# Moving a matmul chain forward, splitting a normalization root in two, and asking for weights on ScalarE's queue

## The chip, the cores and the metric

The kernel runs on one core of a Trainium2 chip. The metric is the device time of one execution in microseconds (us), as the median of several runs. TensorE (PE) does the matrix products, VectorE (DVE), ScalarE (ACT) and GpSimd (POOL) the elementwise work, and SyncE (SP) issues most DMAs.

## The reference

Everything is float32. `x` is 2 x 1024 tokens of 512 features.

```python
xn = layernorm(x)                                # over the 512 features
K  = s4_kernel(Lambda, p, q, B, Ct, step, 512)   # 512 values, real
s  = irfft(rfft(xn, 1024) * rfft(K, 1024))[:512] + D * xn   # causal convolution along the features
h1 = xn @ w1.T + 2 * (xn @ A1.T) @ B1.T          # hidden size 1376, LoRA rank 16
h3 = xn @ w3.T + 2 * (xn @ A3.T) @ B3.T
g  = silu(h1) * h3
f  = g @ w2.T + 2 * (g @ A2.T) @ B2.T
out = x + s * silu(f)
```

## The kernel before

The 2048 tokens are four blocks of TB = 512, each of four tiles of 128. Blocks 0 and 1 form super-block sb 0, blocks 2 and 3 form sb 1. Features lie on the partitions after a transpose on TensorE (`transpose`, pass L332; its copies out of PSUM are L340, L342 and L343 on ScalarE). The hidden units are cut into 11 chunks: five pairs of 128-unit chunks (NPAIR = 5) and a last one of 96.

The first half, h1, h3 and the gate, is done with Strassen-Winograd products: a 2 x 2 block product takes seven products instead of eight, at the price of sums of weights and of tokens. For a pair this is done at two levels, so there are seven chains of seven steps each. The steps of a chain have the numbers 1, 6, 2, 7, 5, 3, 4; each product (L812) writes one of the PSUM banks `x`, `w`, `y`. `Chain.step` snapshots bank `x` on ScalarE (L832) after steps 6 and 5, copies it to bank `w` after step 1 (L850), and adds bank `y` on VectorE (L836). `got` then combines the chain's results with those of other chains (L926, on VectorE or GpSimd), `Gate` applies silu (L885, ScalarE) and the product (L893, GpSimd), and `store_g` writes the result to DRAM by SyncE's queue (L864). The intermediate values lie in rotating buffers: `value("s")` has 10 and `value("c")` has 4; the pair's sums lie in `ua_one` and others.

The sums that the products need are these. `outer_weight_sums` (L486) and `inner_weight_sum` (L498) add blocks of weights, `outer_token_sum` (L374) and `inner_token_sum` (L387 to L393) blocks of tokens, all on VectorE with both operands in SBUF. The LoRA term is not a separate pass: `lora_product` (L429) multiplies the two factors into PSUM, and `merge` (L439, VectorE) adds them to the loaded weight. `load_pair` (L448) loads a pair's weights with four DMAs, two of `w1T` and two of `w3T`.

The normalization needs a mean, a variance and a reciprocal root for each token. Block 2's statistics are made by VectorE (L252, L253), block 3's by ScalarE (`act_sums` L259, `act_squares` L270) with small steps on GpSimd (L265, L266, L279). `pool_root` (L289 to L302) is a chain of 14 small GpSimd operations that gives scale and shift for blocks 2 and 3 together, and `normalize` applies them to a tile on ScalarE (L321) or on GpSimd (L325).

The order is written out by hand: `at(place, what)` puts an event on a heap, and all events are issued in order of place. One unit of place is about one TensorE product, `add_chain(n, ...)` puts a chain into slot n, that is at 7 n plus the places of its steps, and `after(delay, what)` adds an event behind the current one. Each engine works off its instructions in the order in which they were issued, and SyncE its DMA requests too, each behind the waits of those before it.

The last phase (out of the scope of most of the change) multiplies by w2 and the convolution. `conv_product` makes the causal 512 x 512 Toeplitz product of a 128-token tile from blocks of 128 columns (L986); the fp32 product of one block is two passes of TensorE.

Of the kernel before, what the change touches and what calls it, by code (L numbers as in the profile page):

```python
# [12 lines left out]
F32 = mybir.dt.float32  # L13
# [4 lines left out]
P = 128  # L18
# [89 lines left out]
def s4_gated_ffn(  # L108
# [59 lines left out]
    def bank(tag, borrow=False):  # L168

        i = turn[tag]  # L170
        if not borrow:
            turn[tag] = 1 - i
        return psum.tile([P, 512], F32, tag=f"{tag}{i}", name=tag, bufs=1)

    def aux():
        return bank("aux")
# [36 lines left out]
    ]  # L213

    def value(tag="s"):
        return upool.tile([P, TB], F32, tag=tag, name=tag, bufs={"s": 10, "c": 4}[tag])


    events, now = [], [0.0]
# [219 lines left out]
        nc.vector.scalar_tensor_tensor(to, ps, LORA_SCALE, to, mult, add)  # L439


    def load_pair(c):
        w = wpool.tile([P, 8, 2, 2, P], F32, tag="w", name="w")
        for v, src in enumerate((w1T, w3T)):
            for half in range(2):
                slot = (1, 2, 0, 3)[2 * v + half]
                rows = src[half * HALF : (half + 1) * HALF, PAIR_AT[c] : PAIR_AT[c] + 2 * P]
                nc.sync.dma_start(  # L448
                    out=w[:, slot].rearrange("p k m h -> p k (m h)"),
                    in_=rows.rearrange("(k p) h -> p k h", p=P),  # L450
                )
        return w
# [8 lines left out]
    def merge_half(w, half, v, ps):  # L461
        merge(w[:, (1, 2, 0, 3)[2 * v + half]].rearrange("p k m h -> p (k m h)"), ps[v])

    def merge_whole_pair(c, w, first=None, delays=(1.15, 2.3, 4.3, 4.4)):

        ps = [first or [bank("y", True), bank("w", True)], [bank("aux"), bank("aux")]]
        for half in range(2):
            for k in range(2):
                for v in range(2):
                    n = slice(half * 2 * P, (half + 1) * 2 * P)  # L470
                    lora_product(
                        ps[k][v][:, n], 2 * k + v, 2 * half + k, PAIR_AT[c], 2 * P, half == 0
                    )
        for (k, v), when in zip(((0, 0), (0, 1), (1, 0), (1, 1)), delays):
            to = w[:, (slice(1, 3), slice(0, 4, 3))[v], k].rearrange("p s m h -> p s (m h)")
            from_ = ps[k][v].rearrange("p (s n) -> p s n", s=2)
            after(when, lambda to=to, from_=from_: merge(to, from_))
# [418 lines left out]
    def last_chain(ab, sb):  # L896
        a, gate = ab, Gate(LASTR, LAST, sb)

        def pairs(i):
            n = B_AT[i]  # L900
            b = xr[:, n, sb] if n < 3 else xt[:, n - 3, sb]
            return [(a[A_AT[i]][:, k, :], b[:, k, :]) for k in range(2)]

        def got(o, c):
            if o < 20:
                gate.put(o, value("c")[:LASTR, :], c)
            else:
                gate.put(o, c)

        return Chain(pairs, LASTR, lambda o: value(), got, 1, 2 if sb == 0 else 1)  # L910

    def pair_chains(c, w, s, order):


        st = {}

        def at(name, o):
            key, n = (name + "_one", o - 11) if o < 20 else (name + "_three", o - 21)
            if key not in st:
                st[key] = upool.tile(  # L920
                    [P, 2, TB], F32, tag=key, name=key, bufs=2 if key == "ua_three" else 1
                )
            return st[key][:, n, :]

        def plus(o, to, a, b):
            (nc.vector if o < 20 else nc.gpsimd).tensor_tensor(to, a, b, add)  # L926

        def chain(j):
            gate = (
                Gate(P, 2 * c + (j in (5, 4)), int(j in (5, 3))) if j in (2, 5, 3, 4) else None  # L930
            )
            early3 = j == 3 and order.index(3) < order.index(5)
            if early3:
                st["early3"] = (gate, {})

            def pairs(i):
                return [(weight_operand(w, s, i, j), token_operand(i, j))]

            def keep(o):
                if j == 1 or j == 7 and o > 20:  # L940
                    return at("ua" if j == 1 else "u3", o)
                return value()

            def got(o, m):
                ua = at("ua", o)
                if j == 1:
                    if o < 20:
                        nc.scalar.copy(ua, m)
                elif j == 6:
                    plus(o, ua, ua, m)  # L950
                elif j == 7:
                    plus(o, at("u3", o), ua, m)
                elif early3:
                    held = st["early3"][1]
                    held[o] = m
                    if o < 20:
                        held[o] = value("c")
                        nc.scalar.copy(held[o], m)
                else:
                    if j == 5:  # L960
                        plus(o, ua, ua, m)
                    t = value("c") if o < 20 else m
                    plus(o, t, ua if j in (2, 3) else at("u3", o), m)
                    gate.put(o, t)
                    if j == 5 and "early3" in st:
                        g3, held = st["early3"]
                        plus(o, held[o], held[o], ua)
                        g3.put(o, held[o])

            return Chain(pairs, P, keep, got, 0.7 if (c, j) == (NPAIR - 1, order[5]) else 0)  # L970

        return [chain(j) for j in order]
# [6 lines left out]
    def conv_product(lhs, x01, x12, sb, tok, tag):  # L979
# [18 lines left out]
        m = work.tile([P, DIM], F32, tag="m", name="m", bufs=2)  # L998
        nc.scalar.copy(m[:, : 3 * P], shared[:, : 3 * P])
        nc.scalar.copy(m[:, 3 * P :], shared[:, :P])  # L1000
        mul(y, 0, x0, k0, True)
        mul(y, 3, x0, k3)
        mul(y, 1, x01[sb][:, tok], k2)
        mul(y, 2, x12[sb][:, tok], k1)
        mul(y, 3, x321, k0)
# [65 lines left out]
    mv = norm_tile(1)  # L1071
    norm_stats(1, range(NTT))
    norm_root(mv, 1)
    mv_late = norm_tile(2, 3)
    ab_last = last_operands(w_last, s_last)


# [25 lines left out]
    add_chain(3, lambda: last_chain(ab_last, 1), PLACES)  # L1103
    for n in range(2, 7):

        add_chain(n + 2, pair_chain(0, n), AT_T2 if n == 2 else PLACES)
    for c in range(1, NPAIR):
        for n in range(7):

            hurry = (c, n) in ((NPAIR - 2, 6), (NPAIR - 1, 4))  # L1110
            places = SOON if hurry else PLACES
            if (c, n) == (NPAIR - 1, 5):
                places = (*PLACES[:-1], (4, 13.5))
            add_chain(2 + 7 * c + n, pair_chain(c, n), places)
    at(-10, lambda: normalize(1))
    at(-9.9, lambda: last_sums(w_last, s_last))
    at(-10.5, lambda: ps_pair.append(pair_products(0, 1, [aux(), aux()])))
# [13 lines left out]
    for tt in range(NTT):  # L1131
        at(-0.4 + 0.1 * tt, lambda tt=tt: norm_stats(2, (tt,)))
        at(-1.4 + 0.1 * tt, lambda tt=tt: act_sums(3, tt))
        at((-0.3, -0.2, 1.7, 1.8)[tt], lambda tt=tt: act_squares(3, tt))
    at(-0.9, lambda: act_means(3))
    at(1.9, lambda: act_variances(3))
    at(6.9, lambda: pool_root(mv_late, 2, 3))
    at(7.7, lambda: normalize(2))
    at(8, lambda: normalize(3, (0,)))
    for n, place in enumerate((12.1, 12.8, 13.7, 14.4)):  # L1140
        b, i = divmod(n, 2)
        at(place, lambda b=b, i=i: transpose(2 + b, range(2 * i, 2 * i + 2)))
    for name, when in ((3, 15.7), (2, 15.9), (1, 21.2), (4, 21.4)):
        at(when, lambda name=name: outer_token_sum(1, name))
    at(18, other_factors)
    at(22.5, spill)
    for name, when in ((1, 12.7), (2, 13.4), (4, 14), (3, 30.5)):
        at(when, lambda name=name: inner_weight_sum(w_pair[0], s_pair[0], name))
    for name, raw, when, *half in (
        (3, True, 21.6),  # L1150
        (2, True, 22.8),
        (3, False, 24.2),
        (2, False, 30.2),
        (1, True, 34.4),
        (1, False, 37.5, 0),
        (1, False, 40.3, 1),
        (4, True, 47.6),
        (4, False, 50.2, 0),
        (4, False, 52.3, 1),
    ):  # L1160
        at(when, lambda of=(name, raw, *half): inner_token_sum(*of))

    for c in range(NPAIR):
        t0 = 14 + 49 * c

        def ready(j):

            n = orders[c].index(j)
            return 7 * (n + (2 if c == 0 and n > 1 else 0)) + (0 if c == 0 else t0) + 13.3

        if c + 1 < NPAIR:
            nx = c + 1
# [2 lines left out]
                return lambda: what(nx, w_pair[nx], *args)  # L1175

            if c > 0:
                at(t0 + 7.5, lambda nx=nx: w_pair.update({nx: load_pair(nx)}))
            t1 = t0 + (24 if c == 0 else 16)
            if c == 0:  # L1180
                at(
                    5.7,
                    lambda nx=nx: merge_whole_pair(
                        nx, w_pair[nx], [bank("w"), bank("w")], (4.1, 4.2, 4.8, 5.8)
                    ),
                )
            else:
                at(t0 + 15.6, step(merge_whole_pair))
            for n, name in enumerate((3, 2, 1, 4)):
                at(  # L1190
                    14.5 + 0.2 * n if c == 0 else t1 + 8.5 + 1.5 * n,
                    lambda nx=nx, name=name: outer_weight_sums(w_pair[nx], (name,)),
                )
            for name, when in (
# [462 lines left out]
```

## Time and profile before

| | us |
|---|---|
| median of 3 runs | 441.27 (441.01 to 441.75) |
| profiled execution | 442.36 |
| its span in the trace | 440.6 |

The granted TensorE clock is 0.999. The profile is of one execution. A row of a group gives line, engine, operation, output and input names, shape and count; the timeline gives start and duration in us, and in square brackets the idle time just before the row and what ended it. DVE, ACT, POOL and SP are the engines above, `SPq` is SyncE issuing a DMA, and `PEld` is the load of a weight into TensorE. Busy times of the engines, in shares of the span: PE 98%, DVE 72%, POOL 48%, ACT 33%. DMA moves 53.6 MB, 122 GB/s on average.

### The profile page before, as it was taken

To read this page: it belongs to the slowest core of one execution; us is meant where nothing else is said; L and a number is where in the kernel's file an instruction comes from. 1 tells how busy PE (TensorE), PEld (TensorE's weight loads), DVE (VectorE), ACT (ScalarE), POOL (GpSimd) and SP (SyncE) were. 2 spreads that over 40 slices of the span, in tenths; PEclk is the share of its full clock that TensorE was granted. 3 is DMA by queue.
4 is the path that set the end of the run, shared out by engine and by line. 5 is a ranking of instruction groups with operands and counts; after the bars stand their busy time and mean duration, and the time that the engine had idled before them with its cause. 6 is when DMAs were issued, how large, how long until landed. Compare 5 with 4: busy or idle time off the path is not lost.

```text
span 440.6 us, 5150 instructions
## 1 busy us (share of the span) xinstructions
PE 433.3 (98%) x1696; PEld 268.0 (61%) x1696; DVE 317.9 (72%) x519; ACT 144.8 (33%) x298; POOL 212.8 (48%) x174
## 2 busy tenths in 40 slices
PE   8999999999999999999999999999999999999996
PEld 7535334443444444444443446888898999999996
DVE  5889999955885687468745796979786885653234
ACT  3767242453255324532453242211101212112121
POOL 2539177994689468945894468400000122222221
PEclk9999999999999999999999999999999999999999
DMA  8920304025002500250045426395901842322211
GB/s 257 368 76 19 138 1 149 24 71 162 31 25 86 154 24 25 89 170 25 24 131 205 160 95 216 94 361 193 345 31 73 289 136 95 144 95 97 76 68 48
DMA packets 35465, 53.60 MB, mean 122 GB/s; under 512 B 4688, under 2 KB 21520, under 8 KB 35312
## 3 DMA queue, kind: packets, MB, share of 16 engines
q1 hardware_dynamic: 35088, 52.69, 35.7%
q10 hardware_dynamic: 352, 0.60, 0.4%
q8 instruction: 13, 0.21, 0.2%
q14 instruction: 12, 0.10, 0.1%
HBM read 33.88 MB, written 19.40 MB: 121 GB/s over the span
## 4 chain that ended last, share of the span: by engine, by line
PE 89%; DVE 7%; DMA 2%; ACT 1%; issue 1%; SPq 0%; POOL 0%; DVEq 0%; POOLq 0%; ACTq 0%
PE x L812 43%; PE y L812 23%; PE w L812 12%; PE aux L986 4%; PE w L986 2%; PE w L1047 1%; DMA w<-in_w1T_dram 1%; DVE xt L374 1%; DVE w L486 1%; DVE s L498 1%; DVE w L439 1%; PE y L429 1%; PE y L585 1%; PE aux L767 1%; DVE aux L1372 1%
## 5 line engine op out<-in xcount | busy, mean ns | idle before, releaser
L1375 POOL TENSOR_TENSOR o<-o,xin 128x512 f32<-128x512 f32 (+1 forms) x17 | 23.2, 1366 | 133.0 <-DVE o L1374 128.1
L893 POOL TENSOR_TENSOR s<-c,s 128x512 f32<-128x512 f32 (+1 forms) x44 | 64.1, 1464 | 15.4 <-ACT c L885 13.0
L832 ACT COPY s<-x 128x512 f32<-128x512 f32 (+1 forms) x54 | 31.5, 584 | 84.4 <-PE x L812 84.3
L812 PE MATMUL x<-t_in,s 128*128 128x512 f32 (+1 forms) x148 | 55.4, 501 | 0.0
L836 DVE TENSOR_TENSOR s<-s,y 128x512 f32<-128x512 f32 (+1 forms) x54 | 36.1, 680 | 14.7 <-PE y L812 8.8
L926 POOL TENSOR_TENSOR s<-ua_three,s 128x512 f32<-128x512 f32 x20 | 32.0, 1602 | 25.0 <-DVE s L836 24.8
L812 PEld LDWEIGHTS x<-t_in,s 128*128 128x128 f32 x148 | 26.6, 190 | 23.3 <-issue 11.5
L926 POOL TENSOR_TENSOR ua_three<-ua_three,s 128x512 f32<-128x512 f32 x20 | 30.6, 1528 | 13.9 <-DVE s L836 13.9
L812 PE MATMUL y<-t_in,s 128*128 128x256 f32 (+1 forms) x108 | 35.9, 459 | 0.9 <-DVE w L439 0.9
L1397 ACT COPY z<-x 128x256 f32<-128x256 f32 x24 | 8.8, 371 | 70.2 <-PE x L812 70.2
L885 ACT ACTIVATE c<-c 128x512 f32<-128x512 f32 x40 | 25.2, 632 | 14.2 <-DVE c L926 14.2
L926 POOL TENSOR_TENSOR s<-u_three,s 128x512 f32<-128x512 f32 x20 | 28.7, 1437 | 1.8 <-ACT c L885 1.0
L1372 DVE TENSOR_TENSOR aux<-aux,m 128x384 f32<-128x384 f32 x32 | 18.1, 565 | 15.8 <-PE aux L986 14.2
L812 PEld LDWEIGHTS y<-t_in,s 128*128 128x128 f32 x108 | 20.1, 190 | 12.4 <-issue 8.8
L850 ACT COPY w<-x 128x512 f32<-128x512 f32 (+1 forms) x37 | 21.2, 572 | 10.8 <-PE x L812 10.7
L926 POOL TENSOR_TENSOR u_three<-ua_three,u_three 128x512 f32<-128x512 f32 x10 | 15.6, 1556 | 15.0 <-DVE u_three L836 15.0
L812 PE MATMUL x<-t_in,w 128*128 128x512 f32 x40 | 20.9, 605 | 0.0
L812 PE MATMUL x<-xr,w 128*128 128x512 f32 x40 | 20.7, 616 | 0.1
L812 PE MATMUL x<-xt,w 128*128 128x512 f32 x40 | 20.6, 597 | 0.0
L812 PE MATMUL x<-xr,s 128*128 128x512 f32 x40 | 20.5, 614 | 0.0
L812 PE MATMUL x<-xt,s 128*128 128x512 f32 x40 | 20.4, 592 | 0.0
L486 DVE TENSOR_TENSOR w<-w 128x512 f32<-128x512 f32 x20 | 19.7, 991 | 0.2
(329 smaller groups left out, 917.1 us busy)
## 6 DMA issues: line engine op xcount, KB each, us to landing
g_dram<-s SPq DMA_DIRECT2D x40, 256.0 KB, 2.1
g<-g_dram SPq DMA_DIRECT2D x10, 512.0 KB, 6.0
xin<-in_x_dram SPq DMA_DIRECT2D x16, 256.0 KB, 2.7
out_dram<-o SPq DMA_DIRECT2D x14, 256.0 KB, 2.0
t_in<-g_dram SPq DMA_DIRECT2D x6, 512.0 KB, 3.9
w<-in_w1T_dram SPq DMA_DIRECT2D x10, 256.0 KB, 4.1
w<-in_w3T_dram SPq DMA_DIRECT2D x10, 256.0 KB, 4.6
t_in<-in_x_dram SPq DMA_DIRECT2D x8, 256.0 KB, 5.6
```

What stands on the lines that cost most here:

```text
L486: nc.vector.tensor_tensor(*sums[name])
L812: nc.tensor.matmul(ps[:, cols], lhsT=lhsT, rhs=rhs if parts == 1 else rhs[:, cols], start=first and i == 0 and part == 0, stop=i == len(pa ...
L832: nc.scalar.copy(t, self.x)
L836: nc.vector.tensor_tensor(t, t, self.y, add)
L850: nc.scalar.copy(self.w, self.x)
L885: nc.scalar.activation(c, c if src is None else src, AF.Silu)
L893: nc.gpsimd.tensor_tensor(g, act, g, mult)
L926: (nc.vector if o < 20 else nc.gpsimd).tensor_tensor(to, a, b, add)
L986: nc.tensor.matmul(to[:, n * P : (n + 1) * P], lhsT=x_, rhs=by, start=start, stop=True, skip_group_check=True,)
L1372: nc.vector.tensor_tensor(y[:, P:], y[:, P:], m[:, n * P : (n + 3) * P], add)
L1375: (nc.vector if last else nc.gpsimd).tensor_tensor(o, o, self.xin[h][:, cols], add)
L1397: nc.scalar.copy(t, xb)
```

## The change

1. The first chain of pair 1, `pair_chain(1, 0)`, goes from slot 9 to slot 4. Chains 2 to 6 of pair 0 move one slot later. The buffers of `ua_one` are doubled, those of value "s" go from 10 to 8. The merge of pair 1 takes other banks, its outer weight sums are spread over 14.5 to 30, and pair 0's inner token sums and its inner weight sum 3 come later, the token sums in halves.
2. Blocks 2 and 3 each get a `pool_root` of their own (28 small operations in place of 14), block 2's at place 1.85. All four tiles of block 2 are normalized by ScalarE, all four of block 3 by GpSimd. Block 2's transposes are one TensorE row earlier.
3. In the last chain of sb 0, `late` is 0 instead of 1.
4. The weights of pairs 2 to 4 are requested by ScalarE's queue, and pair 2's merge is 7 places later.
5. In `conv_product`, two matmuls of 128 columns become one with a strided output and operand of 256.

```diff
-        return upool.tile([P, TB], F32, tag=tag, name=tag, bufs={"s": 10, "c": 4}[tag])
+        return upool.tile([P, TB], F32, tag=tag, name=tag, bufs={"s": 8, "c": 4}[tag])
...
-    def load_pair(c):
+    def load_pair(c, queue=nc.sync):
...
-                nc.sync.dma_start(
+                queue.dma_start(
...
-    def merge_whole_pair(c, w, first=None, delays=(1.15, 2.3, 4.3, 4.4)):
-
-        ps = [first or [bank("y", True), bank("w", True)], [bank("aux"), bank("aux")]]
+    def merge_whole_pair(c, w, first=None, delays=(1.15, 2.3, 4.3, 4.4), tag="aux"):
+
+        ps = [first or [bank("y", True), bank("w", True)], [bank(tag), bank(tag)]]
...
-        return Chain(pairs, LASTR, lambda o: value(), got, 1, 2 if sb == 0 else 1)
+        return Chain(pairs, LASTR, lambda o: value(), got, sb, 2 if sb == 0 else 1)
...
-                    [P, 2, TB], F32, tag=key, name=key, bufs=2 if key == "ua_three" else 1
+                    [P, 2, TB], F32, tag=key, name=key, bufs=2 if key[:2] == "ua" else 1
...
-        mul(y, 0, x0, k0, True)
-        mul(y, 3, x0, k3)
+        nc.tensor.matmul(
+            y.rearrange("p (n t) -> p n t", t=P)[:, 0::3],
+            lhsT=x0,
+            rhs=conv[:, :DIM].rearrange("p (n t) -> p n t", t=P)[:, 0::3],
+            start=True,
+            stop=True,
+            skip_group_check=True,
+        )
...
-    mv_late = norm_tile(2, 3)
+    mv_late = norm_tile(2), norm_tile(3)
...
-        add_chain(n + 2, pair_chain(0, n), AT_T2 if n == 2 else PLACES)
+        add_chain(n + 3, pair_chain(0, n), AT_T2 if n == 2 else PLACES)
...
-            add_chain(2 + 7 * c + n, pair_chain(c, n), places)
+            add_chain(4 if (c, n) == (1, 0) else 2 + 7 * c + n, pair_chain(c, n), places)
...
-        at((-0.3, -0.2, 1.7, 1.8)[tt], lambda tt=tt: act_squares(3, tt))
+        at((-0.3, 1.65, 1.7, 1.8)[tt], lambda tt=tt: act_squares(3, tt))
...
-    at(6.9, lambda: pool_root(mv_late, 2, 3))
-    at(7.7, lambda: normalize(2))
-    at(8, lambda: normalize(3, (0,)))
-    for n, place in enumerate((12.1, 12.8, 13.7, 14.4)):
+    at(1.85, lambda: pool_root(mv_late[0], 2))
+    at(6.9, lambda: pool_root(mv_late[1], 3))
+    at(9, lambda: normalize(2, range(NTT)))
+    at(9.1, lambda: normalize(3, ()))
+    for n, place in enumerate((10.7, 11.7, 13.7, 14.4)):
...
-    for name, when in ((1, 12.7), (2, 13.4), (4, 14), (3, 30.5)):
+    for name, when in ((1, 12.7), (2, 13.4), (4, 14), (3, 37.5)):
...
-        (3, False, 24.2),
-        (2, False, 30.2),
-        (1, True, 34.4),
-        (1, False, 37.5, 0),
-        (1, False, 40.3, 1),
-        (4, True, 47.6),
-        (4, False, 50.2, 0),
-        (4, False, 52.3, 1),
+        (3, False, 24.5, 0),
+        (3, False, 28.6, 1),
+        (2, False, 31, 0),
+        (2, False, 33, 1),
+        (1, True, 40.2),
+        (1, False, 43.5, 0),
+        (1, False, 46.3, 1),
+        (4, True, 51.6),
+        (4, False, 54.2, 0),
+        (4, False, 57.3, 1),
...
-            return 7 * (n + (2 if c == 0 and n > 1 else 0)) + (0 if c == 0 else t0) + 13.3
+            return 7 * (n + (3 if c == 0 and n > 1 else 0)) + (0 if c == 0 else t0) + 13.3
...
-                at(t0 + 7.5, lambda nx=nx: w_pair.update({nx: load_pair(nx)}))
-            t1 = t0 + (24 if c == 0 else 16)
+                at(t0 + (8.1 if c > 1 else 15.1), lambda nx=nx: w_pair.update({nx: load_pair(nx, nc.scalar)}))
+            t1 = t0 + (24, 22, 16, 16)[c]
...
-                        nx, w_pair[nx], [bank("w"), bank("w")], (4.1, 4.2, 4.8, 5.8)
+                        nx, w_pair[nx], [aux(), aux()], (3.2, 3.3, 4.8, 5.8), "w"
...
-                at(t0 + 15.6, step(merge_whole_pair))
+                at(t0 + (15.6 if c > 1 else 22.6), step(merge_whole_pair))
...
-                    14.5 + 0.2 * n if c == 0 else t1 + 8.5 + 1.5 * n,
+                    (14.5, 23, 25, 30)[n] if c == 0 else t1 + 8.5 + 1.5 * n,
```

## The prediction

> **What bounds the kernel now.** First the page's engine busy times and its chain, then TensorE's own waits, then its timeline for the places where a pass starts late, then the engines that it waited for. The page says which engine carries the time:
>
> ```profile
> PE 433.3 (98%) x1696; PEld 268.0 (61%) x1696; DVE 317.9 (72%) x519; ACT 144.8 (33%) x298; POOL 212.8 (48%) x174
> PE 89%; DVE 7%; DMA 2%; ACT 1%; issue 1%; SPq 0%; POOL 0%; DVEq 0%; POOLq 0%; ACTq 0%
> ```
>
> TensorE is busy for 98% of the span, so the time is its work plus the stalls between its passes; what no pass waits for is free. The waits list names the long ones only (total, times, longest):
>
> ```profile
> PE y L812 <- DVE w L439: 0.9, 1, 0.9
> PE x L812 <- DVE xt L374: 0.2, 1, 0.2
> ```
>
> The short stalls come from TensorE's timeline. One pass over 512 columns starts 0.43 us after the last, over 256 columns 0.216, over 128 columns 0.112; what a start lags beyond that is a stall.
>
> ```profile
> 25.81 0.59 PE L812 MATMUL x<-xt,w 128*128 128x512 f32 x1
> 26.56 1.93 PE L812 MATMUL x<-xt,last 128*96 128x512 f32 x4 [0.16 <-issue]
> ...
> 104.14 1.02 PE L812 MATMUL w<-t_in,s 128*128 128x512 f32 x2
> 106.05 1.13 PE L812 MATMUL y<-t_in,s 128*128 128x512 f32 x2 [0.89 <-DVE w L439]
> ```
>
> So 26.56 is 26.56 − 25.81 − 0.43 = 0.32 late, and 106.05 is 106.05 − 104.14 − 0.86 = 1.05 late. Read this way up to 106 us, and leaving out lags of 0.1 that recur throughout, the stalls are: 20.18 0.31; 26.56 0.32; 35.92 0.30; 37.44 0.07; 47.09 0.33; 55.06 0.21; 56.26 0.23; 82.75 0.17; 106.05 1.05. After 106 there are none.
>
> **Part 4, weights by ScalarE's queue.** SyncE's queue shows why the merge (L439) of pair 2 is late:
>
> ```profile
> 99.18 0.36 SPq L864 DMA_DIRECT2D g_dram<-s  x1
> 99.63 0.96 SPq L448 DMA_DIRECT2D w<-in_w1T_dram  x2
> 101.76 0.37 SPq L864 DMA_DIRECT2D g_dram<-s  x1
> 102.18 1.00 SPq L448 DMA_DIRECT2D w<-in_w3T_dram  x2
> ```
>
> The queue waits for GpSimd's gate product before each store (L864), so the two w3T requests leave 2.5 us after the two of w1T; the page's landing times are 4.1 us and 4.6 us. The change moves these four off that queue, and pair 2's merge seven products (about 6 us) later, so that its LoRA products stand 8 products (6.9 us) after the last use of the buffer instead of about one. Requests then go out some 3.6 us earlier relative to the products, and the 1.05 goes with about 2.5 us to spare. ScalarE pays 4 issues of 0.48 to 0.5 (0.96/2, 1.00/2), so 1.95 us, at three pairs. What stands behind them on ScalarE is the next snapshot (L832) after step 1: its operand is ready 3.7 to 4.2 us after that step, TensorE wants the bank at 5.15. The requests wait on stores that have landed 3.5 us before, so I cost them at 0; without this cover each pair would pay up to 1.95.
>
> A rule of the Trainium skill speaks against this part: "DMA: Bandwidth & Descriptors", section "Issuing engines are not separate DMA queues", says that issuing from several engines adds no bandwidth and saves only the sequencer's issue time. By it alone nothing on the path is saved, and the sum would be 1.05 worse; the rows above show an issue held by a store's wait, which the rule does not count.
>
> **Part 5, one strided conv pass.** Sixteen conv products lose two 128-column passes for one of 256, twice each (fp32 runs two passes): 16 × (4 × 0.1117 − 2 × 0.2156) = 0.25 saved, if a strided operand streams at the same rate. No such row exists; the pass reads the same two runs of 128 columns as the two it replaces, which excludes a loss, so the bounds are 0 and 0.25. I take 0.25, by the nearest row, the contiguous 256-column passes.
>
> **Part 1, chain (1,0) in slot 4.** It adds no passes. Products that need no inner token sum now fill the stretch where the others were waited for: 47.09 (L374), 55.06 (VectorE's L926 queued behind L389), 56.26 (L832 behind it), 82.75: 0.33 + 0.21 + 0.23 + 0.17 = 0.94 saved. New hazards are the value buffers, 8 instead of 10 (the stores land at least 8 us before a reuse), and the split token sums at about 66 and 71 us; I find slack at both and cost them at 0 (bound 0.7, the length of an L926 or L836 queued ahead).
>
> **Part 3** moves L885 ahead of the L358 copies: 20.18 grows by 0.05. With act_squares(3,1) moved 2 places later, the snapshot at 26.56 is no longer queued behind two L270 of 0.72: 0.32 saved.
>
> **Part 2, two roots.** The stalls at 35.92 and 37.44 (0.37) lie at rows that change and go. What comes instead is read from GpSimd and VectorE now:
>
> ```profile
> 27.96 0.79 POOL L279 TENSOR_SCALAR mv<-act_sums 128x4 f32<-128x4 f32 x1 [3.34 <-ACT c L270]
> 28.83 0.53 POOL L289 TENSOR_SCALAR veps<-mv 128x8 f32<-128x8 f32 x1
> 29.45 0.24 POOL L290 TENSOR_SCALAR shift<-mv 128x8 f32<-128x8 f32 x1
> 29.77 0.20 POOL L291 TENSOR_SCALAR rs_y<-veps 128x8 int32<-128x8 int32 x1
> ...
> 32.92 0.20 POOL L302 TENSOR_TENSOR shift<-shift,rs_y 128x8 f32<-128x8 f32 x1
> ```
>
> ```profile
> 26.87 0.66 DVE L486 TENSOR_TENSOR w<-w 128x512 f32<-128x512 f32 x1
> 27.45 1.22 DVE L374 TENSOR_TENSOR xt<-xr,xt 128x1024 f32<-128x1024 f32 x1
> 28.59 0.68 DVE L486 TENSOR_TENSOR w<-w 128x512 f32<-128x512 f32 x1
> ```
>
> A root op lasts 0.20, one each 0.285. L279 and L289 last until VectorE's sum of two SBUF operands ends (28.67, 29.27): one small op passes per such sum. Root 2 may start at 27.06 (its statistics end at 26.95), is held by all three sums to 29.4, and then needs 11 × 0.285: 32.54. ScalarE's first tile is ready after 0.81, at about 33.39, the next 0.72 later. TensorE wants them one row earlier than now, at 33.03 − 0.27 = 32.76. It loses 0.68 for the first tile, 0.25 for the second, 0.26 at the next transposes, which wait for the copies that free their bank (0.58 each, behind L885): 1.19. If the small ops slipped between the sums, root 2 would end at 31.1 and only 0.26 stay.
>
> Root 3 follows at 32.6: its first op is held by the inner weight sum (L498) to 33.9, the other 13 need 3.7, to about 37.8. Then VectorE's next two L498, at about 37.16 and 38.24, meet the last two ops, due at 37.21 and 37.5: a tie. TensorE reaches block 3's transposes at 39.2. (a) If the ops slip ahead, tile 0 runs beside L498 at 1.59 (the two L325 at 34.75 and 36.33 did, against 0.77 alone), ready at 39.38; tile 1, with a sum over half of it, takes 1.18 (between 0.77 and 1.59), ready at 40.55 where 39.83 is wanted: 0.18 + 0.72 = 0.90. At 0.77 each there would be 0. (b) If each op is held by one L498, tile 0 is ready at 40.65, tile 1 at 41.42 for 41.10: 1.45 + 0.32 = 1.77; with tile 1 at 1.59 it is 2.6. I take (a), since VectorE's L498 waits behind an L836 that waits for TensorE, delayed here itself, while GpSimd waits for nobody.
>
> "Trainium Architecture — The Big Picture", section "What this means for kernel authors", calls the port pair of VectorE and GpSimd an exclusive lock. By that rule (b) is the case, and the sum would be 0.87 to 1.7 worse; the L325 at 33.99 kept its 0.77 although an L498 began at 34.27, so a started op is not always held.
>
> **The sum**: saved 1.05 + 0.25 + 0.94 + 0.32 + 0.37 − 0.05 = 2.88; lost 1.19 + 0.90 = 2.09; net −0.79. The profiled execution took 442.36 (span 440.6, 1.76 outside it); after it would take 441.57. It lies 1.09 above the median 441.27, so the median becomes 440.5.
>
> **Rivals.**
> A. GpSimd is not held: root 2 ends near 31.1, block 3 loses 0 to 0.9, so −2.88 + 0.26 + (0 to 0.9) = −2.6 to −1.7: 438.7 to 439.6. For it: the whole root in 4.3 us in the trace. Against: L279's 0.79.
> B. GpSimd is held at block 3, (b): +0.08 to +0.91, and with tile 0 at 1.59 as well (0.82 more) +1.73: 441.4 to 443.0. It decides for slower than the measurement can tell (0.88 us, 0.2%) once block 3 stalls for over 3.76 − 1.19 = 2.57. For it: the 0.79 and 0.53 rows.
> C. ScalarE's four issues take longer than the 1.95: the snapshot slips past 5.15 − 4.2 + 1.95 = 2.9 us; doubled to 3.9, it costs 1.0 at each of three pairs: −0.79 + 3.0 = +2.2, 443.5. Against: SyncE's rows.
> D. The conv pass gains nothing, or a token sum at 66 to 71 us comes late: −0.79 + 0.25 + 0.7 = +0.16 to, with more than one, about +1.
>
> **Chances.** Forecast 0.36 (split by its 0.45 to 1.33 in block 3: faster 0.14, same 0.22); A 0.28 (faster 0.27, same 0.01); B 0.26 (same 0.10, slower 0.16); C 0.06 (slower); D 0.04 (slower). Faster 0.41, same 0.33, slower 0.26. The forecast's own range is 440.0 to 440.9. The range over cases runs from 439.0 (most of A) to 442.8 (most of B).
>
> **What would show it.** Right: no stall near 106; L448 of pairs 2 to 4 on ScalarE's queue at about 0.48 each; 256-column passes at L1001 with 0.216 pitch; stalls of 0.7 near 33 and under 1 near 39 to 41, GpSimd's root ops stretched beside L486, L374 and L498. Wrong: a block 3 stall of 2 or more (B), none at 33 (A), a snapshot late after the issues (C), or stalls between 41 and 82 that this count lacks.

## The result: slower by 0.35%

The changed kernel takes 443.47 us (442.56 to 444.85, 9 runs) against 441.75 us (440.85 to 443.36, 9 runs): a ratio of 1.0035 with a 95% interval of 1.002 to 1.0051, or 0.9 to 2.3 us slower. The forecast was 440.5 us, counted from 441.27, the median of the first three of these nine runs of before. The profiled execution took 443.21 us with a span of 441.4; the one of before had 442.36 and 440.6, so the two traces differ by 0.85 us where the medians differ by 1.72. The rest of that gap has a cause of its own, shown below. Where the text says "at full clock", it compares the spans of executions with a mean granted clock of 0.998 or more, since the traces at 0.992 to 0.996 show a stretch at a lower clock (0.65 from 12 to 16 us in a_no2_sq, 0.52 from 67 to 70 us in a_sums_far).

First the engine row of the page of after: TensorE is busy for 0.4 us less than before, and the kernel is still longer, so the loss is idle time.

```profile
PE 432.9 (98%) x1664; PEld 267.2 (61%) x1664; DVE 312.3 (71%) x521; ACT 145.7 (33%) x299; POOL 215.3 (49%) x187
```

TensorE's waits (total, times, longest) say where: the transposes L332 wait for GpSimd's tiles of block 3 and for ScalarE's tiles of block 2. The two L812 rows shown of before are gone.

```profile
PE aux L332 <- POOL t_in L325: 1.9, 1, 1.9
PE aux L332 <- ACT s L321: 0.8, 1, 0.8
PE aux L332 <- ACT t_in L321: 0.5, 1, 0.5
```

Counting late starts as the prediction did, the stalls of after are: 20.35 0.32; at block 2 33.51 0.68, 34.21 0.21 and 36.57 0.15; at block 3 41.31 2.04 and 42.07 0.26; 62.78 0.18; 90.89 0.17. The stalls of before at 26.56, 35.92, 37.44, 47.09, 55.06, 56.26 and 106.05 have no counterpart.

GpSimd's timeline shows the end of root 3 (start, duration), and VectorE's below it the same stretch:

```profile
36.73 1.64 POOL L299 TENSOR_TENSOR rs_t<-rs_t,veps 128x4 f32<-128x4 f32 x1
38.45 1.06 POOL L300 TENSOR_SCALAR rs_t<-rs_t 128x4 f32<-128x4 f32 x1
39.60 0.49 POOL L301 TENSOR_TENSOR rs_y<-rs_y,rs_t 128x4 f32<-128x4 f32 x1
40.17 0.20 POOL L302 TENSOR_TENSOR shift<-shift,rs_y 128x4 f32<-128x4 f32 x1
```

```profile
36.62 0.68 DVE L836 TENSOR_TENSOR s<-s,y 96x512 f32<-96x512 f32 x1 [2.60 <-PE y L812]
37.23 1.08 DVE L498 TENSOR_TENSOR s<-s,w 128x896 f32<-128x896 f32 x1
38.34 1.09 DVE L498 TENSOR_TENSOR s<-w,s 128x896 f32<-128x896 f32 x1
39.35 0.68 DVE L486 TENSOR_TENSOR w<-w 128x512 f32<-128x512 f32 x1
```

The ends match: L299 ends at 38.37 and the first L498 at 38.31; L300 at 39.51 and the second L498 at 39.43; L301 at 40.09 and L486 at 40.03. Three operations of 0.2 us took 3.2 us, while VectorE had stood idle for 2.60 us just before. The four tiles then took 3.03 us, 0.77 each, with no sum of two SBUF operands beside them.

### The profile page after: what moved, and what is told of

Same layout as the page of the kernel before. It is cut to its first block, busy times and chain, and to the rows that moved or that the text cites. A ratio compares the mean times of both kernels' runs of the same rounds, so it can differ in the third digit from the quotient of the medians.

```text
span 441.4 us, 5099 instructions
## 1 busy us (share of the span) xinstructions
PE 432.9 (98%) x1664; PEld 267.2 (61%) x1664; DVE 312.3 (71%) x521; ACT 145.7 (33%) x299; POOL 215.3 (49%) x187
## 4 chain that ended last, share of the span: by engine, by line
PE 90%; DVE 4%; POOL 3%; DMA 1%; issue 1%; ACT 1%; SPq 0%; DVEq 0%; POOLq 0%
PE x L812 45%; PE y L812 23%; PE w L812 12%; PE aux L986 2%; PE w L986 2%; PE aux L1001 2%; DMA s<-in_x_dram 1%; DVE stats L252 1%; PE y L429 1%; PE y L585 1%; PE aux L767 1%; PE aux L332 1%; DVE xt L374 1%; DVE aux L1381 1%; POOL rs_t L299 0%
## 5 line engine op out<-in xcount | busy, mean ns | idle before, releaser
L812 PE MATMUL x<-t_in,s 128*128 128x512 f32 (+1 forms) x148 | 55.4, 500 | 0.0
L836 DVE TENSOR_TENSOR s<-s,y 128x512 f32<-128x512 f32 (+1 forms) x54 | 36.4, 681 | 21.0 <-PE y L812 13.2
L926 POOL TENSOR_TENSOR s<-ua_three,s 128x512 f32<-128x512 f32 x20 | 30.2, 1512 | 21.5 <-DVE s L836 21.5
L812 PEld LDWEIGHTS x<-t_in,s 128*128 128x128 f32 x148 | 26.8, 190 | 22.4 <-issue 12.4
L812 PE MATMUL y<-t_in,s 128*128 128x256 f32 (+1 forms) x108 | 35.8, 458 | 0.0
L885 ACT ACTIVATE c<-c 128x512 f32<-128x512 f32 x40 | 25.2, 632 | 9.6 <-DVE c L926 9.4
L812 PEld LDWEIGHTS y<-t_in,s 128*128 128x128 f32 x108 | 20.2, 190 | 11.1 <-issue 9.1
L812 PE MATMUL x<-t_in,w 128*128 128x512 f32 x40 | 21.0, 606 | 0.0
L812 PE MATMUL x<-xr,w 128*128 128x512 f32 x40 | 20.7, 611 | 0.0
L812 PE MATMUL x<-xt,w 128*128 128x512 f32 x40 | 20.6, 597 | 0.0
L812 PE MATMUL x<-xr,s 128*128 128x512 f32 x40 | 20.5, 614 | 0.0
L812 PE MATMUL x<-xt,s 128*128 128x512 f32 x40 | 20.4, 592 | 0.0
L812 PE MATMUL y<-xt,w 128*128 128x512 f32 x40 | 19.9, 592 | 0.0
```

What stands on the lines that cost most here:

```text
L812: nc.tensor.matmul(ps[:, cols], lhsT=lhsT, rhs=rhs if parts == 1 else rhs[:, cols], start=first and i == 0 and part == 0, stop=i == len(pa ...
L836: nc.vector.tensor_tensor(t, t, self.y, add)
L885: nc.scalar.activation(c, c if src is None else src, AF.Silu)
```

## The experiments

The times below are medians, each beside the runs of the kernel before on the same chip.

| kernel | us | before, same chip | ratio, interval |
|---|---|---|---|
| a_no_part2 | 440.98 | 442.03 | 0.9981, 0.9965 to 0.9998 |
| b_part2 | 445.31 | 442.03 | 1.0072, 1.0046 to 1.0097 |
| a_sums_late | 443.48 | 442.03 | 1.003, 1.0012 to 1.0048 |
| a_spqueue | 443.69 | 442.03 | 1.0029, 1.0013 to 1.0045 |
| a_sums_far | 446.21 | 441.46 | 1.0096, 1.0073 to 1.012 |
| a_far_tr | 445.54 | 441.46 | 1.0075, 1.0049 to 1.0102 |
| b_merge_late | 441.74 | 441.46 | 1.0005, 0.9992 to 1.0017 |
| b_actq | 441.79 | 441.46 | 0.9999, 0.9987 to 1.0011 |
| a_dve3 | 442.37 | 442.06 | 1.0015, 0.9999 to 1.0032 |
| a_no2_sq | 440.93 | 442.06 | 0.998, 0.9967 to 0.9992 |
| a_no2_s1 | 440.66 | 441.67 | 0.9975, 0.9955 to 0.9994 |

Names with a_ start from the changed kernel, names with b_ from the kernel before.

### Is it the two roots? a_no_part2 and b_part2

```diff
# a_no_part2, against the changed kernel (b_part2 is the reverse, and act_squares(3,1) at 1.65, against the kernel before)
-    mv_late = norm_tile(2), norm_tile(3)
+    mv_late = norm_tile(2, 3)
-    at(1.85, lambda: pool_root(mv_late[0], 2))
-    at(6.9, lambda: pool_root(mv_late[1], 3))
-    at(9, lambda: normalize(2, range(NTT)))
-    at(9.1, lambda: normalize(3, ()))
-    for n, place in enumerate((10.7, 11.7, 13.7, 14.4)):
+    at(6.9, lambda: pool_root(mv_late, 2, 3))
+    at(7.7, lambda: normalize(2))
+    at(8, lambda: normalize(3, (0,)))
+    for n, place in enumerate((12.1, 12.8, 13.7, 14.4)):
```

> The changed kernel with its two roots undone: one pool_root for blocks 2 and 3 at place 6.9, normalizing and block 2's transposes where they were before; everything else as changed. Theory 1 (the root's small GpSimd operations are held by VectorE's SBUF sums, and that is all that makes the change slow): TensorE's stalls at block 2 (0.68, 0.21, 0.15) and at block 3 (2.04, 0.26), 3.34 us together, go, and at most the 0.37 of before at these rows returns, so about 3.0 us under the changed kernel and 1.3 or more under the kernel before. Theory 2 (the loss lies elsewhere, in the start or in the later chains): under 1 us better than the changed kernel.

> The kernel before with the two roots alone (and act_squares(3,1) two places later). Theory 1: the stalls of 0.7 to 1.0 us at block 2 and 2 to 2.3 us at block 3 come here too, less the 0.32 at 26.56 and the 0.37 at 35.92 and 37.44 of before: 2.3 to 2.9 us slower than the kernel before. Theory 2: within 1 us of the kernel before.

Without the two roots the changed kernel is 2.5 us faster by the medians, and faster than the kernel before. The two roots alone make the kernel before 3.3 us slower. Theory 1 holds in both directions. Both amounts differ from what was expected. In a_no_part2 two stalls of 0.44 and 0.96 us are at 35.9 and 37.8 where the kernel before has 0.30 and 0.07 (taken up below). In b_part2 the stall at block 3 is 3.42 us, because seven of the root's operations are held there; two of them, from GpSimd's timeline of b_part2:

```profile
34.40 1.04 POOL L293 TENSOR_TENSOR rs_t<-rs_t,veps 128x4 f32<-128x4 f32 x1
35.53 1.03 POOL L294 TENSOR_SCALAR rs_t<-rs_t 128x4 f32<-128x4 f32 x1
```

They end at 35.44 and 36.56, each within 0.06 us of the end of one of the two L498 that run at 34.30 to 35.38 and 35.42 to 36.51. The 3.3 us of b_part2 is a balance: in its trace the passes after the stall of 3.42 us ran at half clock and lost about 1.6 us more, a stall of 0.96 stands at pair 2's merge (taken up below), and the stalls of before at 47.09, 55.06, 56.26 and 82.75 (0.94 together) are gone.

### Is it the sums beside the root? a_sums_late, a_sums_far, a_far_tr

```diff
# a_sums_late, against the changed kernel
-    for name, when in ((1, 12.7), (2, 13.4), (4, 14), (3, 37.5)):
+    for name, when in ((1, 12.7), (2, 14.6), (4, 15.2), (3, 37.5)):
# a_sums_far, against the changed kernel
-    for name, when in ((1, 12.7), (2, 13.4), (4, 14), (3, 37.5)):
+    for name, when in ((1, 12.7), (2, 15.5), (4, 29), (3, 37.5)):
-                    (14.5, 23, 25, 30)[n] if c == 0 else t1 + 8.5 + 1.5 * n,
+                    (18, 23, 25, 30)[n] if c == 0 else t1 + 8.5 + 1.5 * n,
# a_far_tr: a_sums_far, and
-    for n, place in enumerate((10.7, 11.7, 13.7, 14.4)):
+    for n, place in enumerate((12.1, 12.8, 13.7, 14.4)):
```

> The changed kernel with two inner weight sums of pair 0 (L498, names 2 and 4) issued at 14.6 and 15.2 instead of 13.4 and 14, so that VectorE has no SBUF sum of theirs between 37 and 39.4 us, when root 3 runs; nothing else changes. Theory 1 (held by the sums): root 3's last four operations take 0.2 each, block 3's tile 0 is ready near 39.0 and its stall falls from 2.3 to under 0.5; 1.8 to 2.3 us under the changed kernel. Rival (root 3 starts too late, whatever VectorE does, or the one L486 left holds it as long): the stall stays over 1.5.

a_sums_late missed: its stalls at block 3 are 1.24 and 1.09, no less in sum than in the changed kernel. The edit had moved too little. The L486 and one L498 came forward into the place of the sums that were moved, and a second L498 fell on the second tile. Its GpSimd timeline has two rows that were not expected:

```profile
36.80 0.66 POOL L299 TENSOR_TENSOR rs_t<-rs_t,veps 128x4 f32<-128x4 f32 x1
37.55 1.54 POOL L300 TENSOR_SCALAR rs_t<-rs_t 128x4 f32<-128x4 f32 x1
```

L299 ends at 37.46, 0.07 after an L836 (36.70 to 37.39), whose one operand lies in PSUM and behind which an L486 follows at once; and L300 lasted through that L486 and an L498 on end (37.31 to 39.00), not through one.

> The changed kernel with all three of VectorE's SBUF sums that met root 3 taken out of its way: pair 0's inner weight sums 2 and 4 at 15.5 and 29 (13.4 and 14 before this edit), pair 1's first outer weight sum at 18 (14.5). Theory 1 (root 3's operations are held by these sums, one operation for each sum): the last operations of root 3 take 0.2 each, the root ends near 37.9 instead of 40.4 and block 3's stall falls from 2.3 to 0.3 or less; 2.0 us under the changed kernel, that is 0 to 0.8 under the kernel before. Rival (root 3 only starts too late): the stall stays at 1 or more.

With the sums out of the way, the same operations in GpSimd's timeline of a_sums_far, and VectorE beside them (all rows of this trace lie 1.4 us later than in the changed kernel, from its start on):

```profile
38.14 0.20 POOL L299 TENSOR_TENSOR rs_t<-rs_t,veps 128x4 f32<-128x4 f32 x1
38.42 0.23 POOL L300 TENSOR_SCALAR rs_t<-rs_t 128x4 f32<-128x4 f32 x1
38.73 0.20 POOL L301 TENSOR_TENSOR rs_y<-rs_y,rs_t 128x4 f32<-128x4 f32 x1
```

```profile
38.04 0.68 DVE L836 TENSOR_TENSOR s<-s,y 96x512 f32<-96x512 f32 x1 [2.60 <-PE y L812]
```

Block 3's stall is gone from TensorE's timeline altogether. That settles the cause of the stall: VectorE's sums held the root. The same L836 alone, with no sum behind it (VectorE's next row starts at 40.88), held nothing: L299 began 0.10 us after it and took 0.20. The time grew all the same, to 446.21 us, since VectorE has no room for these sums later. Here are its timeline, the start that TensorE gave late behind it, and what the clock did next (the windows: stretch, length, busy time of TensorE, weight loads, VectorE, ScalarE, GpSimd with counts, granted clock, DMA):

```profile
60.68 2.16 DVE L498 TENSOR_TENSOR s<-w,s 128x896 f32<-128x896 f32 x1
62.76 1.75 DVE L486 TENSOR_TENSOR w<-w 128x512 f32<-128x512 f32 x1
64.43 0.67 DVE L836 TENSOR_TENSOR s<-s,y 96x512 f32<-96x512 f32 x1
```

```profile
65.15 2.47 PE L812 MATMUL y<-xt,last 128*96 128x512 f32 x4 [2.09 <-DVE s L836]
```

```profile
60.00:65.00 5.00, 3.07 (x8) 1.04 (x6) 5.00 (x4) 1.55 (x3) 4.92 (x3) 1.00 0.02 6
67.00:70.00 3.00, 3.00 (x5) 1.01 (x3) 1.93 (x2) 0.59 (x1) 0.83 (x1) 0.52 0.56 142
```

The L498 (1.08 alone) took 2.16 and the L486 (0.66 to 0.68 alone) 1.75, both beside GpSimd's gate operations: the sums are held too. The L836 behind them, which adds bank y and so frees it, let TensorE go on 2.25 us late. After that stall the granted clock was 0.52 from 67 to 70 us, and four passes of 0.43 took 0.85 each, for another 1.65 us.

> The kernel of a_sums_far with block 2's transposes one TensorE row later again, at 12.1 and 12.8 as before the change. Theory 1: block 2's first tile, ready at 33.45, is then wanted at about 34.4, so the stalls of 0.68 and 0.21 go too; with block 3's gone, 2.8 to 3.2 us under the changed kernel, 1.3 to 1.6 under the kernel before. Rival (the later transposes only move the stall to the copies out of PSUM on ScalarE, behind its four normalized tiles): 0.5 to 1 us of stalls stay at 34 to 38, and it gains under 0.5 over a_sums_far.

a_far_tr has the same stalls near 56 and 64 us (1.21 and 2.25, and the half clock). Its stalls at 36 to 39 are 0.69 and 0.16, where a_sums_far had 0.68, 0.21 and 0.15, so the stalls stay, as the rival said. What they wait for is not what it said: the 0.69 ends on L885, the silu that reads bank `x` behind the four tiles on ScalarE (35.40 to 35.97), and not on a copy of the transposes.

```profile
36.02 1.13 PE L812 MATMUL x<-xr,w 128*128 128x512 f32 x2 [0.53 <-ACT c L885]
```

The medians differ by 0.67, more than the rival's 0.5. But four of a_far_tr's six executions and five of a_sums_far's are under full clock, and those at full clock have spans of 441.7 and 442.2 against 442.0; the stalls here differ by 0.19.

### Another engine for root 3: a_dve3

```diff
# against the changed kernel
-    at(6.9, lambda: pool_root(mv_late[1], 3))
+    at(12.72, lambda: norm_root(mv_late[1], 3))
-    at(9.1, lambda: normalize(3, ()))
+    at(12.73, lambda: normalize(3, (1,)))
```

> The changed kernel with block 3's root on VectorE (ten small operations, in its idle 34 to 36.6 us) instead of GpSimd, and one of block 3's four tiles normalized by ScalarE. Theory 1 (what costs is that root 3 runs on GpSimd beside VectorE's sums): the root takes about 2.0 us, block 3's stall falls from 2.3 to 0.2 to 0.9 us; 1.4 to 2.1 us under the changed kernel, nothing new after 46 us since VectorE's order is otherwise kept. Rival (VectorE has no room for it, as with the sums moved to 15.5 and 29): new stalls of 1 us or more between 45 and 72 us.

On VectorE the root takes 1.94 us (35.19 to 37.13, ten operations of 0.16), in time that was idle, and block 3's stall falls from 2.30 to 0.39. At full clock the spans have a median of 440.05 against 441.5 of the changed kernel: 1.45 us less, at the low end of what was expected, since the small stalls of before near 57 us return (0.12 and 0.23).

### Is it ScalarE's queue? a_spqueue, b_merge_late, b_actq

```diff
# a_spqueue, against the changed kernel
-... load_pair(nx, nc.scalar) ...
+... load_pair(nx) ...
# b_merge_late, against the kernel before
-            t1 = t0 + (24 if c == 0 else 16)
+            t1 = t0 + (24, 22, 16, 16)[c]
-                at(t0 + 15.6, step(merge_whole_pair))
+                at(t0 + (15.6 if c > 1 else 22.6), step(merge_whole_pair))
# b_actq, against the kernel before (and load_pair's queue as in the change)
-                at(t0 + 7.5, lambda nx=nx: w_pair.update({nx: load_pair(nx)}))
+                at(t0 + 8.1, lambda nx=nx: w_pair.update({nx: load_pair(nx, nc.scalar)}))
```

> The changed kernel with the weights of pairs 2 to 4 requested by SyncE's queue again, at the same places and with pair 2's merge still 7 places later. Theory A (the later merge alone takes the 1.05 us stall away): no stall over 0.2 at pair 2's merge near 113 us, time within 0.3 us of the changed kernel. Theory B (the queue matters): the two w3T requests leave 2 to 2.5 us later than on ScalarE's queue and a stall of 0.5 to 1.1 us comes back at pair 2's merge.

> The kernel before with pair 2's merge 7 places later (22.6 instead of 15.6, its later weight sums with it) and nothing else; the requests stay on SyncE's queue. Theory A (the later merge alone takes the stall away): no stall at the merge, about 1.05 us faster than the kernel before. Theory B (the queue was needed too): a stall of 0.3 or more stays.

> The kernel before with the weights of pairs 2 to 4 requested by ScalarE's queue at t0 + 8.1, the merge where it was. Theory A (the w1T request waits for the buffer of pair 0, so its landing of 4 to 5 us sets the end whichever queue asks): the stall near 106 us stays at 0.6 to 1.05 us, time within 0.4 us of the kernel before. Theory B (SyncE's waits for stores cause the stall): it falls under 0.3 and the kernel is about 0.9 us faster. Should ScalarE wait for the buffer itself, snapshots behind it come late and the time grows by 0.5 us or more.

In a_spqueue SyncE's queue asks for the weights with a store in between, as it did before:

```profile
107.78 0.46 SPq L448 DMA_DIRECT2D w<-in_w3T_dram  x1
108.89 0.37 SPq L864 DMA_DIRECT2D g_dram<-s  x1
109.31 0.46 SPq L448 DMA_DIRECT2D w<-in_w3T_dram  x1
```

No stall comes of it, and its spans at full clock have a median of 441.55 against 441.5 with ScalarE's queue. The queue makes no difference that can be measured. Nor does anything else of part 4: b_merge_late and b_actq have no stall at the merge, and yet neither is faster than the kernel before. That contradicts a saving of 1.05 us, and so the kernel before was traced again.

### Was the stall at 106 us always there? before_again, before_again2

> The kernel before once more, unchanged, for a second trace. Theory 1 (the 1.05 us stall at pair 2's merge is in every execution): a stall of 0.9 to 1.1 us near 106 us again, span near 440.6. Theory 2 (it was in the first traced execution and is missing in most, so that nothing was saved there): no stall over 0.3 us near 106 and a span of 439.3 to 440.1, as most of the other executions of this kernel at a clock of 0.998 or more have.

> The kernel before a third time, for the same question: theory 1 a stall of 0.9 to 1.1 us near 106 us, theory 2 none over 0.3 us.

Neither trace has it, though the requests leave in the same order. The execution of before_again still took 442.12 us (span 440.3, outside the 439.3 to 440.1 that theory 2 expected), that of before_again2 441.20 (439.4). Against before_again2, the trace of before_again is 0.3 us late from its start on and has another stall, of 0.55 at 237.36, behind a merge that waited for a DMA of w2T. The two passes in the timeline of before_again2 follow each other at the usual 0.86 us:

```profile
104.15 1.02 PE L812 MATMUL w<-t_in,s 128*128 128x512 f32 x2
105.01 1.02 PE L812 MATMUL y<-t_in,s 128*128 128x512 f32 x2
```

VectorE's first merge of pair 2, in before_again2 and then in the first trace of before:

```profile
103.83 0.69 DVE L439 SCALAR_TENSOR_TENSOR w<-y,w 128x512 f32<-128x512 f32 x1 [2.02 <-DMA w<-in_w1T_dram]
```

```profile
105.30 0.69 DVE L439 SCALAR_TENSOR_TENSOR w<-y,w 128x512 f32<-128x512 f32 x1 [3.51 <-DMA w<-in_w1T_dram]
```

The first w1T request went out at 99.63 in both. The merge started 1.47 us later in the first trace, because the data of the same DMAs landed later: the slower of the two w1T transfers took 5.1 us from issue to landing in the first trace, 3.3 us in before_again2 and 3.2 us in before_again. Most executions of the kernel before at full clock have spans of 439.1 to 440.1 (median 439.85 beside a_dve3), and the first traced one had 440.6: it was one with a late landing. b_part2's trace also has a stall there (0.96) and a landing of 5.1 us, so it is one that some executions have. How many have it isn't known.

### What is left without part 2: a_no2_sq, a_no2_s1

```diff
# a_no2_sq: a_no_part2, and
-        at((-0.3, 1.65, 1.7, 1.8)[tt], lambda tt=tt: act_squares(3, tt))
+        at((-0.3, -0.2, 1.7, 1.8)[tt], lambda tt=tt: act_squares(3, tt))
# a_no2_s1: a_no2_sq, and
-    for name, when in ((1, 12.7), (2, 13.4), (4, 14), (3, 37.5)):
+    for name, when in ((1, 13.2), (2, 13.4), (4, 14), (3, 37.5)):
```

> The kernel a_no_part2 with act_squares(3,1) at -0.2 again, so that nothing of part 2 is left and parts 1, 3, 4 and 5 stand alone. Theory 1 (the joint root in a_no_part2 starts 1 us later than in the kernel before because it waits for that squares pass, and that makes its two stalls of 0.44 and 0.96 us at 35.9 and 37.8): the root starts near 28.9, the two stalls shrink to 0.4 together, the 0.32 at 26.5 comes back; 0.5 to 0.8 us under a_no_part2 and 1.2 to 1.8 under the kernel before. Rival (the stalls come from L885 now ahead in ScalarE's queue, not from the start of the root): they stay, and the time is that of a_no_part2 plus 0.3.

The stalls stayed, 0.45 and 0.96, and the time is that of a_no_part2 (440.98), so theory 1 was wrong: the place of the squares pass doesn't make them. (The stall at 26.5, and with it the 0.3 us that the rival counted for it, didn't return either.) In a_no2_sq's timelines, the last operation of the joint root, and TensorE:

```profile
34.35 0.99 POOL L302 TENSOR_TENSOR shift<-shift,rs_y 128x8 f32<-128x8 f32 x1
```

```profile
38.13 1.13 PE L812 MATMUL x<-xr,w 128*128 128x512 f32 x2 [0.80 <-ACT c L885]
```

In the changed order of merges, VectorE reaches its first L498 (34.20 to 35.28) before the root has ended, and that sum holds L302; in the kernel before the root ended at 33.12 and this L498 began at 34.27. a_no2_s1 moves this one sum behind the L836 that follows it.

> The kernel a_no2_sq (part 2 undone altogether) with pair 0's inner weight sum 1 issued at 13.2 instead of 12.7, behind the total of bank y. It asks why stalls of 0.45 and 0.96 us stay in a_no2_sq where the kernel before has 0.30 and 0.07. Theory 1 (the last operation of the joint root, held 0.99 by this one sum, makes ScalarE's tiles and L885 behind them late): that operation takes 0.2, both stalls shrink to 0.5 together or less, and the kernel is 0.5 to 0.9 us under a_no2_sq, about 439.9 to 440.4. Rival (ScalarE's order at these rows sets it): both stalls stay and the time is that of a_no2_sq within 0.3.

```profile
33.33 0.20 POOL L302 TENSOR_TENSOR shift<-shift,rs_y 128x8 f32<-128x8 f32 x1
```

```profile
36.33 1.13 PE L812 MATMUL x<-xr,w 128*128 128x512 f32 x2 [0.53 <-ACT c L885]
```

All rows of a_no2_sq lie 1.0 us later than here, from its start on. L302 takes 0.20 and the stalls fall by 0.72, from 1.41 to 0.69. The 0.69 is the wait for L885, which stands behind three tiles on ScalarE: that part belongs to the rival. At full clock the span is 438.8 against 439.05. The difference to a_no2_sq is smaller than was expected; a new stall of 0.17 at 60.23 takes back a part of it. Against the kernel before the version is at 0.9975 (0.9955 to 0.9994), 1.0 us faster, and 440.66 against 443.47 us of the changed kernel. It is the fastest that was run.

## Why the prediction was wrong

The forecast's sum was −0.79. Term by term, from the traces of before and after:

- **Block 3, taken at 0.90, was 2.04 + 0.26 = 2.30.** This is the larger of two steps that failed. The prediction saw the tie of root 3's last operations with two L498 and chose case (a), in which they slip ahead. Case (b), with 1.77 to 2.6, was true. The argument for (a) was that L498 waits behind an L836 that waits for TensorE, while GpSimd waits for nobody. VectorE did wait, for 2.60 us, but it didn't help: L299 started at 36.73, before the first L498, and should have been through at 36.93. It started 0.11 us after that L836 and ended only after the L498 that followed at once. So three operations were held instead of two (b) or none (a).
- **Block 2, taken at 1.19, was 0.68 + 0.21 + 0.15 = 1.04.** The reading of the hold at root 2, of the first tile (33.39 forecast, 33.45 measured) and of the first stall (0.68 and 0.68) was right. The wait for the copies was smaller, 0.15 instead of 0.26.
- **The 1.05 at 106 us** is the other step that failed. The stall went from the trace, as forecast, but two more traces of the kernel before don't have it, and b_merge_late and b_actq, without it, are no faster than the kernel before. Read against the median, the term was about 0. Its reading was off too: the pass at 106.05 waited for the merge of w1T, which was requested at 99.63 and landed late, and not for the w3T requests that left 2.5 us behind. The prediction even noted that its profiled execution lay 1.09 us over the median, and subtracted that as if it were an offset of the same size for both kernels; it was for the most part a stall of this one execution.
- **Part 1, taken at 0.94, was 0.77 less 0.18.** 47.09, 55.06 and 56.26 went. The 0.17 at 82.75 is now at 90.89, and a new 0.18 is at 62.78: bank y was freed by an L836 that ended at 62.73, queued behind one of the pair 1 sums that the change spread out, an L486 that took 1.76 at 60.38.
- **Part 3's and the squares' 0.32 − 0.05, and the 0.37 at 35.92 and 37.44** came as forecast, but for the 0.05: the stall at 20.18 grew from 0.31 to 0.32.
- **The conv passes**: the page has 32 fewer TensorE passes, as the count said. In the trace of after these 32 passes of L1001 last 0.217 us each from start to start, beside 0.112 for the ones of 128 columns, so a strided operand streams at about the rate of a contiguous one here, and 64 × 0.1117 − 32 × 0.217 = 0.20 us is saved. That is too small to be seen among the times.

Corrected by block 3 (+1.40), block 2 (−0.15) and part 1 (+0.35), the sum against the traces is −0.79 + 1.60 = +0.81, where 0.85 was measured. Without the 1.05 it is +1.86 against the medians, where 1.72 was measured, with an interval of 0.9 to 2.3.

Of the rivals, B was the one that happened, at the place and, for block 3, the price that it was given (2.30, within 1.77 to 2.6). Its 441.4 to 443.0 us still missed the measured 443.47, as it too counted the 1.05 as saved (2.57 was its point of decision for block 3; without the 1.05 any stall over 1.5 decides). Rival C was excluded: after has the requests on ScalarE's queue without a late snapshot, and a_spqueue has the same time.

The lock rule that the prediction weighed, in the Trainium skill's "Trainium Architecture — The Big Picture", section "What this means for kernel authors", would have given the better sum. The rows agree with it more than the one L325 that spoke against it: seven root operations in after were held, each to within 0.1 us of the end of a VectorE sum. What the rows add is that a GpSimd operation can be held before the sum itself begins: L299 in after and in a_sums_late began beside an L836, with one operand in PSUM, behind which a sum of two SBUF operands followed at once. The L836 alone doesn't do it, as a_sums_far shows.

## What to carry to other kernels

In these traces each short GpSimd operation of the roots that began while a VectorE sum of two SBUF operands ran lasted to the end of that sum, mostly 0.5 to 1.1 us and at times 1.5 or more, not 0.2 us. So put such a chain where VectorE is idle, or give it to VectorE itself, and count for every sum that can meet it a whole sum, and not that the short operations slip in between. A stall found in one traced execution, above all one that ends on a DMA landing, is not to be counted as a saving until a second trace has it; an execution that lies an unusual distance above the median is a hint that it hasn't. Before moving work off a crowded spot, look for room where it goes: the sums that were moved away from the root cost more at 57 to 65 us than the root's stall had.

## What the runs showed of the hardware that was not expected

- GpSimd operations of 0.2 us were held by two back-to-back VectorE operations for 1.54 us (a_sums_late, L486 and L498), 1.64 (after, L836 and L498) and 1.75 (b_part2, L836 and L498). In other places they got in between two sums, as in after between L498, L498 and L486. What decides it stays open. L836 alone held nothing: in a_sums_far L299 began 0.10 us after one and took 0.20, and L292 in after started at 29.58, beside an L836 from 29.36 to 30.03, and took 0.20. A sum right behind the L836 is not enough either: in b_part2 L299 began at 40.07, 0.22 us after an L836 with an L486 behind it, and took 0.20.
- The hold works both ways: in a_sums_far the L498 of 1.08 took 2.16, and the L486 of 0.68 took 1.75, beside 128x512 operations on GpSimd.
- After an idle stretch TensorE ran at half clock: in a_sums_far the stall ended at 65.15, and the passes took 0.85 instead of 0.43 from 66.6 to 70 (1.65 us lost). a_far_tr lost 1.76 in the same way. In b_part2 the half clock came within 0.5 us of the end of a stall of 3.42 us and lasted 3.3 us (about 1.6 lost); in the changed kernel's trace a stall of 2.04 us brought none. The Trainium skill's "TensorE: Matmul & The Clock Gate", section "Part 1: The HAM clock gate", puts the window in which an idle TensorE loses its clock at about 3.4 us, free-running; a stall of 2.25 us, after one of 1.06 us at 57.3, was enough here. So three stalls of 2.25 to 3.42 us cost 1.6 to 1.8 us beyond themselves, and one of 2.04 cost nothing more; where the limit lies isn't shown.
